# Waiting by tile instead of by pool, early query weights and expert sums in written order, in a two-layer gated cross-attention model

## The chip, the cores and the metric

The kernel runs on one core of a Trainium2 chip. The metric is the device time of one execution in microseconds, and a kernel's time is the median over several executions. Profiled times come from one recorded execution; positions such as "at 2477" are microseconds from the start of its span.

The engines are called by short names: PE is TensorE's matrix multiplication (PEld its weight load), DVE is VectorE, ACT is ScalarE, POOL is GpSimd, and SP is SyncE, whose queue only issues DMAs here. ACT and POOL issue DMAs too.

## What is computed

An input x of 1600 rows (16 sequences of 100) and 512 columns passes four gated stages, all in float32. The second operand is a context of 16 sequences of 722 rows and 384 columns:

```python
x = x + tanh(g_xattn[0]) * attention0(layernorm(x), ctx)   # 16 heads of 32
x = x + tanh(g_ffn[0])   * experts(layernorm(x))           # 8 experts, top 2
x = x + tanh(g_xattn[1]) * attention1(layernorm(x), ctx)   # 8 heads of 64
x = x + tanh(g_ffn[1])   * ffn(layernorm(x))
```

An attention projects x to queries and the context to keys and values, takes a softmax over the 722 context rows for each head, and projects the result back. The experts stage sends every row to its two best experts, each a silu-gated pair of 512x1024 matrices and one of 1024x512, and adds the two results by the weights of a softmax. The last stage normalizes its input again inside, keeps that input as its own residual, and runs a silu network of width 2048 whose weights are int32 numbers with a scale for each group of 128 rows:

```python
def ffn(x):
    h = layernorm(x) * gamma + beta
    w1 = (q1 - 128) * s1          # by groups of 128 rows
    y = silu(h @ w1 + b1)
    w2 = (q2 - 128) * s2
    return x + 0.5 * (y @ w2 + b2)
```

## The kernel before

**Tiles and stages.** The 1600 rows of x stay in SBUF as 13 tiles of up to 128 rows. The stages follow each other on the profile's axis: attention 0 (0 to 959), routing (959 to 1005), experts (1005 to 1633), attention 1 (1634 to 2460), the quantized network (2477 to 2848).

**Who sets the order.** Inside `tc.manual_schedule(engines={PE})` the order of PE's instructions is the order of the program. All other engines get theirs from a scheduler, which may move an instruction ahead of another where data allow. An instruction that `keep_in_program_order` marks stays in written order. So most of this kernel is a list of units written for PE, with the other engines' work placed around it. Buffers come from pools: a tile pool takes a stretch of SBUF or PSUM, and a pool that is opened where an earlier one stood has its first tiles wait for the earlier pool's users. A tag with `bufs=n` turns over n buffers.

**Attention.** `Attention.run` goes through 64 steps, one for each sequence b and each of four column blocks m. In a step PE makes the next step's scores (`ps_s`, L369), attends for the step before (`ps_r` L447 spreads the reciprocals of the softmax sums, `ps_pv` L460 multiplies by the values) and transposes this step's probabilities (`ps_t`, L428). DVE copies the negated scores with their minimum (`ns`, L379 in attention 1), ACT takes their exponential (`pr_a`, L411), and DVE and ACT share the copies of the transposed probabilities (`pT`, L435 and L437). DVE makes the reciprocals (`rinv`, L444) and the scaled result (`tT`, L467). Keys (`ps_k`, L207) and values (`ps_v`, L232) of later sequences fill PE between. `extra[step]` holds units for a given step: `query_input` normalizes a tile of x (`xn_a`, L306 on ACT or L116 on POOL) and transposes it (`ps_tr`, L131), `queries` multiplies by the query weights (`ps_q`, L329), and `project` makes the output (`ps_y`, L473) and adds it to x on DVE (L480). The list `more` gives attention 1 further units.

**Routing and experts.** `Experts` computes logits, the two best experts of every row and a sorted place for each, in a chain of small operations beside which PE makes values of attention 1. Then `slots` runs 29 slots of 128 sorted rows. A slot takes 21.6 us (628 us over 29), multiplies one tile through one expert (`hidden`, then `give`), and loads the weights for the slots ahead on SP's queue (L790 to L794): two of 1 MB for each half of the first pair, and 2 MB for the last matrix. ACT copies the result (`ot`) and writes it to `rows` in DRAM. A branch at L895 for further slots, and one at L1447 for a guarded attention, are not taken with this input.

**Entry to attention 1.** `load_query_weights` fetches Wq on SP (L273), `load_output_weights` fetches Wo on POOL (L282), `output_bias` scales the bias (L300). `combine` gathers a tile's two expert rows from DRAM by indirect DMAs on POOL (`r`, L914) and adds each to x on DVE (L920). `summed` adds that tile's mean and variance (L102, L103) and scales: a square root on ACT (L109), then a reciprocal and a shift on DVE. `sqrt` and `exp` need different tables on ACT, and a change of table shows as ACT_TABLE_LOAD. The first sum stands ahead of attention 1; `more` writes sums 1 to 3 at step 0, and sums 4 to 12 at steps 1 to 9.

**Quantized network.** `quantized_ffn` works on groups of 4, 3, 3 and 3 tiles. `weights` loads integers `q` (one buffer, L961 and L964) and scales into `ffn_w` (L962 and L965), and DVE makes the weights from them (L969). `normal` normalizes twice: POOL makes `xn_ffn` (L116), DVE adds it to x (L983) and takes its moments, POOL normalizes it again, in place. PE transposes it (`ps_hT`, L1004; sixteen transposes for a group of four tiles), DVE scales it (`hT`, L1009), and then PE alternates `ps_y` (L1026) and `ps_z` (L1044) to the end.

Of the kernel before, what the change touches and what calls it, by code (L numbers as in the profile page):

```python
# [8 lines left out]
F32 = mybir.dt.float32  # L9
I32 = mybir.dt.int32  # L10
AF = mybir.ActivationFunctionType
ALU = mybir.AluOpType
AX = mybir.AxisListType
PSUM = bass.MemoryType.PSUM
PE = mybir.EngineType.PE

P = 128
B, T, C = 16, 100, 512
# [30 lines left out]

def bcast(ap, *shape):  # L50
    return ap.to_broadcast(list(shape))


def rows_of(i):
# [80 lines left out]
class Attention:  # L135
# [16 lines left out]
    def open_first(self, ctx):  # L152

        tc, nc, name = self.net.tc, self.net.nc, self.name
        self.pa = ctx.enter_context(tc.tile_pool(name=f"{name}_a", bufs=1))
        self.pk = ctx.enter_context(tc.tile_pool(name=f"{name}_k", bufs=4))
        self.wk = self.pa.tile([P, KK, C], F32, name=f"wk_{name}")
        self.wv = self.pa.tile([P, KK, C], F32, name=f"wv_{name}")
        wk = self.w["Wk"].rearrange("(k p) m -> p k m", p=P)
        t = self.pa.tile([P, KK, S], F32, tag="ctx", bufs=2, name=f"ctx_{name}_0")  # L160
        cx = self.ctxT[0].rearrange("(k p) s -> p k s", p=P)
        for k in range(KK):
            nc.sync.dma_start(self.wk[:, k, :], wk[:, k, :])
            nc.sync.dma_start(t[:, k, :], cx[:, k, :])
        self.cxs[0] = t
        nc.sync.dma_start(self.wv, self.w["Wv"].rearrange("(k p) m -> p k m", p=P))
        if "bk_cols" in self.w:
            self.cols["bk"] = self.pa.tile([P, KC], F32, name=f"bkc_{name}")
            nc.gpsimd.dma_start(self.cols["bk"], self.w["bk_cols"])
# [77 lines left out]

    def open(self, ctx):
        tc, nc, name, w = self.net.tc, self.net.nc, self.name, self.w
        pool = lambda n, k, **kw: ctx.enter_context(  # L250
            tc.tile_pool(name=f"{name}_{n}", bufs=k, **kw)
        )
        self.pb, self.pw, self.p2 = pool("b", 1), pool("w", 1), pool("2", 2)
        self.p3, self.p4 = pool("3", 3), pool("4", 4)
        self.ps_s, self.ps_m = pool("s", 2, space=PSUM), pool("m", 4, space=PSUM)
        self.wq = self.pw.tile([P, KC, C], F32, name=f"wq_{name}")
        self.wo = self.pw.tile([P, KC, C], F32, name=f"wo_{name}")
        for n in ("bq", "bv"):
            if n + "_cols" in w:
                self.cols[n] = self.pw.tile([P, KC], F32, name=f"{n}c_{name}")  # L260
                nc.gpsimd.dma_start(self.cols[n], w[n + "_cols"])
        self.gbo = self.pw.tile([P, C], F32, name=f"gbo_{name}")

        self.tT = self.pw.tile([P, KC, N], F32, name=f"tT_{name}")
        self.probs = [
            self.pw.tile([T, NS * P], F32, name=f"pr{i}_{name}") for i in range(6 if self.G == 4 else 4)
        ]
        for t in self.probs:
            nc.gpsimd.memset(t[:, S:], 0.0)
        self.qT, self.nmax, self.sums, self.negated, self.pT = {}, {}, {}, {}, {}  # L270

    def load_query_weights(self):
        self.net.nc.sync.dma_start(self.wq, self.w["Wq"].rearrange("(k p) m -> p k m", p=P))  # L273

    def load_output_weights(self, queue, pin=False):

# [209 lines left out]
    def run(self, given, after_project=None, more=()):  # L486
# [9 lines left out]
        for g in range(1, B // GB):  # L496
            at = 4 * KC * (g - 1)
            for n, i in enumerate(range(last_tile(g - 1) + 1, last_tile(g) + 1)):
                extra[at + 2 + n].append((self.query_input, i))
            for m in range(KC):  # L500
                extra[at + 7 + 2 * m].append((self.queries, g, m))
        for b in range(B):
# [39 lines left out]
class Experts:  # L542
# [10 lines left out]
    def open(self, pc):  # L553
# [26 lines left out]
            )  # L580
            return t

        self.e_m8 = const_iota([P, NTT, E], [[0, NTT], [1, E]], -E, 0, "e_m8")
        self.j_rows = const_iota([P, E, CAP // P], [[0, E], [P, CAP // P]], 0, 0, "j_rows")
        self.count = const_iota([P, P], [[1, P]], 0, 0, "count")
        self.token = const_iota([P, 2, NTT], [[0, 2], [P, NTT]], 0, 1, "token")
        nc.gpsimd.memset(self.token[NL:, :, NTT - 1], 0.0)
# [41 lines left out]
    def top_two(self, i0, i1):  # L629

        nc, hot = self.net.nc, self.hot
        n, s = i1 - i0, slice(i0, i1)
        lg, at, first, e_m8 = self.lg[:, s], self.at[:, s], self.first[:, s], self.e_m8[:, s]
        for k in range(2):
            nc.vector.tensor_reduce(self.top[:, k, s], lg, AX.X, ALU.max)
            nc.vector.tensor_tensor(
                at, lg, bcast(self.top[:, k, s].unsqueeze(2), P, n, E), ALU.is_equal
            )
            nc.vector.tensor_tensor(at, at, e_m8, ALU.mult)
            nc.vector.tensor_reduce(first, at, AX.X, ALU.min)  # L640
            nc.vector.tensor_tensor(
                hot[:, k, s], e_m8, bcast(first.unsqueeze(2), P, n, E), ALU.is_equal
            )
            if k == 0:
                nc.vector.scalar_tensor_tensor(lg, hot[:, 0, s], -BIG, lg, ALU.mult, ALU.add)
        if i1 == NTT:

            nc.vector.memset(hot[NL:, :, NTT - 1, :], 0.0)
        nc.vector.tensor_tensor(self.sel[:, s], hot[:, 0, s], hot[:, 1, s], ALU.add)
        for i in range(i0, i1):  # L650
            nc.vector.tensor_tensor(
                self.before_tile[:, i + 1, :], self.before_tile[:, i, :], self.sel[:, i, :], ALU.add
            )
# [3 lines left out]
    def places(self, psum, pn):  # L657
# [11 lines left out]
        nc.vector.tensor_scalar(cnt, ps_n, float(CAP), None, ALU.min)  # L669
        more = pn.tile([P, E, CAP // P], F32, name="more")  # L670
        nc.vector.tensor_tensor(
            more, bcast(cnt.unsqueeze(2), P, E, CAP // P), self.j_rows, ALU.is_gt
        )
        ntile = pn.tile([P, E], F32, name="ntile")
        nc.vector.tensor_reduce(ntile, more, AX.X, ALU.add)
# [22 lines left out]
        for k in range(2):  # L698
# [8 lines left out]
        full = of_hot[:, :, :, 1:]  # L707
        nc.vector.tensor_tensor(
            full,
            bcast(rank.unsqueeze(3), P, 2, NTT, E - 1),  # L710
            bcast(self.j_rows[:, 0:1, 1:].unsqueeze(1), P, 2, NTT, E - 1),
            ALU.is_ge,
        )
        fulls = new("fulls")
# [55 lines left out]

    def open_weights(self, ctx, n):

        self.pw[n] = ctx.enter_context(self.net.tc.tile_pool(name=f"moe_w{n}", bufs=1))

    def load(self, j, part, again=False):

# [18 lines left out]

    def open_slots(self, ctx):
        tc = self.net.tc
        pool = lambda n, k, **kw: ctx.enter_context(tc.tile_pool(name=f"moe_{n}", bufs=k, **kw))
        self.p2 = pool("2", 2)
        self.ps_h, self.ps_t = pool("h", 4, space=PSUM), pool("t", 2, space=PSUM)  # L800
        self.ps_o = pool("o", 2, space=PSUM)

    def open_rows(self, ctx):
        self.px = ctx.enter_context(self.net.tc.tile_pool(name="moe_x", bufs=2))

    def gather(self, j, again=False):
        if not again:
# [19 lines left out]
    def hidden(self, j, part):  # L827
# [5 lines left out]
        for n in range(2):  # L833
# [8 lines left out]
                        stop=(k == KC - 1),  # L842
                    )
            phs.append(ph)
        s = self.p2.tile([P, n4, P], F32, tag="silu", name="silu")
        nc.scalar.activation(s, phs[0], AF.Silu)
        m = self.p2.tile([P, n4, P], F32, tag=f"midT{part}", name=f"midT{part}_{j}")
        nc.vector.tensor_tensor(m, s, phs[1], ALU.mult)  # L848
        self.midT[j, part] = m

    def give(self, j):
# [4 lines left out]
        for f in range(KF):  # L856
# [4 lines left out]
                start=(f == 0),  # L861
                stop=(f == KF - 1),
            )
        ot = self.p2.tile([P, C], F32, tag="ot", name=f"ot_{j}")
        nc.scalar.copy(ot, po)
        nc.scalar.dma_start(self.rows[j * P : (j + 1) * P, :], ot)

# [42 lines left out]
    def combine(self, pg, i):  # L910
        net, nc, n = self.net, self.net.nc, rows_of(i)
        for k in range(2):
# [4 lines left out]
                in_=self.rows[:, :],  # L917
                in_offset=bass.IndirectOffsetOnAxis(ap=self.slot_i[:n, k, i : i + 1], axis=0),
            )
            nc.vector.scalar_tensor_tensor(  # L920
                net.x[:n, i, :],
                r[:n, :],
                self.probs[:n, k, i : i + 1],
# [2 lines left out]
                ALU.add,  # L926
            )


def quantized_ffn(net, p, gate, out):  # L930

    nc, tc, x = net.nc, net.tc, net.x
    out = out.rearrange("b t c -> (b t) c")
    with ExitStack() as ctx:
        pool = lambda n, k, **kw: ctx.enter_context(tc.tile_pool(name=f"ffn_{n}", bufs=k, **kw))

        ps, pq, p1, px, ph, p2 = (
            pool("s", 1), pool("q", 1), pool("1", 1), pool("x", 4), pool("h", 2), pool("2", 2),
        )
        ps_t, ps_y, ps_z = (pool(n, k, space=PSUM) for n, k in (("t", 2), ("y", 2), ("z", 4)))  # L940
        small = {}
# [381 lines left out]
def tile_flamingo(ctx: ExitStack, tc: tile.TileContext, a: dict, out: bass.AP):  # L1323
# [21 lines left out]
    with ExitStack() as cm:  # L1345
# [58 lines left out]
        with ExitStack() as c1:  # L1404
# [3 lines left out]
            with ExitStack() as cw:  # L1408
                moe.open_weights(cw, 0)
                moe.open_rows(cw)  # L1410
                with ExitStack() as cr:
                    ps = cr.enter_context(tc.tile_pool(name="route_p", bufs=6, space=PSUM))
                    p2 = cr.enter_context(tc.tile_pool(name="route_2", bufs=2))
                    pn = cr.enter_context(tc.tile_pool(name="route_n", bufs=1))
                    a1.ps_m = ps
                    units = a1.keys_and_values(0)

# [29 lines left out]
                with tc.If(nc.values_load(flag[0:1, 0:1], min_val=0, max_val=1) > 0):  # L1447
                    guarded_attention(net, a["x"], a["ctxT"], w0, tgx[:, 0:1], heads, o_s, x_s)
                    with ExitStack() as cg:
# [17 lines left out]
                            moe.gather(j, again=True)  # L1467
                        moe.weigh()
                        moe.turn_rows(0, ps, again=True)
                with ExitStack() as cs:  # L1470
                    moe.open_weights(cs, 1)
                    moe.open_slots(cs)
                    moe.slots({3: [(a1.load_ctx, 2, True)]})

            a1.open(c1)
            a1.load_query_weights()
            pg = c1.enter_context(tc.tile_pool(name="moe_g", bufs=4))

            def summed(i):
                moe.combine(pg, i)  # L1480
                net.moments(i)
                net.norm_scales(i, i + 1)

            more = []
            for i in range(1, 4):
                more += [(0, summed, i), (1, a1.query_input, i, True), (3, a1.add_bias, i)]
            more += [(3, a1.add_bias, 0)]
            more += [(2, a1.queries, 0, m, T, GT) for m in range(KC)]
            more += [(i - 3, summed, i) for i in range(4, NTT)]
            with tc.manual_schedule(engines={PE}):  # L1490
                summed(0)
                a1.load_output_weights(nc.gpsimd, True)
                a1.output_bias()
                units = a1.keys_and_values(1)[:NS]
                for f, *u in units[:3]:
                    f(*u)
# [65 lines left out]
```

## Time and profile before

| | |
|---|---|
| median of 3 runs | 2849.27 us (2849.23 to 2851.45) |
| profiled execution | 2849.85 us |
| its span | 2848.1 us, mean granted TensorE clock 0.991 |
| PE busy | 2795.5 us, 98% |
| DVE busy | 867.5 us, 30% |
| ACT busy | 864.8 us, 30% |
| POOL busy | 170.6 us, 6% |

"Busy" is the time in which an engine executes instructions; issuing a DMA doesn't count. The profile has several views. The groups list instructions of one line with their count and mean time. The waits list for each engine what ended its idle time, as "instruction <- what it waited for: us in total, times, longest". The chain of waits goes back from the last instruction to what released it. The timeline lists instructions by start time, with start, duration, engine, line, operation, output and inputs, and in square brackets the engine's idle time before and who ended it; a trailing x4 means four of them merged in one row, so that a row's duration is that of all. Table rows of stretches of time give the granted clock, where 1.00 is full speed.

### The profile page before, as it was taken

What the parts mean: (1) busy time and instruction counts of PE and PEld (TensorE: products, weight loads), DVE (VectorE), ACT (ScalarE), POOL (GpSimd) and SP (SyncE); (2) the same over time, 40 slices, a digit from 0 to 9 for tenths busy, and PEclk for the clock granted to TensorE, in tenths of its full rate; (3) what the DMA queues carried; (4) which work ended last, traced back from release to release, by engine and by line L of the source; (5) the groups of instructions that cost most, each with busy time, mean ns of one, the idle gap of its engine ahead of it and who ended that gap; (6) DMA issues with size and microseconds to landing.
All of it is one profiled execution on the core that took longest, in us unless ns stands there. A gap on an engine that the chain in (4) does not pass through costs nothing. (4 is left out here: it accounts for less than half of the span.)

```text
span 2848.1 us, 42495 instructions
## 1 busy us (share of the span) xinstructions
PE 2795.5 (98%) x18000; PEld 1739.8 (61%) x18000; DVE 867.5 (30%) x2569; ACT 864.8 (30%) x1724; POOL 170.6 (6%) x187
## 2 busy tenths in 40 slices
PE   9999999999999999999999979999999999799999
PEld 4555555555556588888788745555555555444554
DVE  4444444444445500000000072233232322521100
ACT  2544454454455310000000033233333333211110
POOL 2000000000000000000000050000000000301000
PEclk9999999999999999999999989999999999899999
DMA  4000000001000489899889441000000000420000
GB/s 160 17 17 17 33 24 24 17 28 33 17 28 1 151 333 330 316 320 320 315 312 320 149 129 32 16 16 32 16 16 32 17 32 1 140 96 15 11 12 9
DMA packets 129880, 278.10 MB, mean 98 GB/s; under 512 B 5824, under 2 KB 5840, under 8 KB 129168
## 3 DMA queue, kind: packets, MB, share of 16 engines
q1 hardware_dynamic: 117888, 246.80, 24.9%
q0 software_dynamic: 5088, 16.28, 1.7%
q10 hardware_dynamic: 6704, 12.19, 1.1%
q8 instruction: 145, 2.38, 0.3%
q14 instruction: 55, 0.45, 0.0%
HBM read 260.31 MB, written 14.94 MB: 97 GB/s over the span
## 5 line engine op out<-in xcount | busy, mean ns | idle before, releaser
L232 PE MATMUL ps_v<-wv_a,ctx_a 128*128 128x512 f32 (+1 forms) x1152 | 524.8, 600 | 2.5 <-ACTq L895 1.6
L207 PE MATMUL ps_k<-ctx_a,wk_a 128*128 128x361 f32 x1488 | 488.6, 473 | 0.0
L837 PE MATMUL ps_h<-xT,w 128*128 128x128 f32 x3712 | 421.1, 276 | 3.7 <-DVEq L1447 3.7
L837 PEld LDWEIGHTS ps_h<-xT,w 128*128 128x128 f32 x3712 | 418.6, 193 | 4.4 <-issue 4.4
L207 PEld LDWEIGHTS ps_k<-ctx_a,wk_a 128*128 128x128 f32 x1488 | 271.9, 190 | 150.4 <-issue 13.5
L232 PEld LDWEIGHTS ps_v<-wv_a,ctx_a 128*128 128x128 f32 (+1 forms) x1152 | 204.7, 185 | 236.9 <-issue 227.2
L392 DVE TENSOR_SCALAR_CACHE_REDUCE ns<-ps_s 100x361 f32<-100x361 f32 x512 | 246.8, 529 | 208.3 <-PE ps_s L369 185.8
L428 PEld LDWEIGHTS ps_t<-ident,pr_a 100*128 100x128 f32 x2304 | 214.0, 141 | 80.5 <-issue 41.6
L411 ACT ACTIVATE pr_a<-ns,extremes 100x722 f32<-100x722 f32 x256 | 227.1, 889 | 71.7 <-DVE extremes L402 71.7
L428 PE MATMUL ps_t<-ident,pr_a 100*128 100x100 f32 x2304 | 237.3, 252 | 1.5 <-DVE rb L455 1.1
L437 DVE COPY pT<-ps_t 128x400 f32<-128x400 f32 x288 | 163.5, 571 | 241.2 <-PE ps_t L428 235.4
L369 PE MATMUL ps_s<-kT_a,qT_a 32*100 32x361 f32 (+1 forms) x1536 | 212.3, 500 | 7.4 <-DVE ns L379 4.8
L239 ACT COPY v_a<-ps_v 128x512 f32<-128x512 f32 x192 | 111.5, 581 | 346.5 <-PE ps_v L232 346.1
L857 PE MATMUL ps_o<-w,midT 128*128 128x512 f32 x464 | 203.9, 592 | 0.0
L379 DVE TENSOR_SCALAR_CACHE_REDUCE ns<-ps_s 100x722 f32<-100x722 f32 x128 | 111.3, 907 | 281.1 <-PE ps_s L369 281.1
L1044 PE MATMUL ps_z<-ffn_w,y_ffn 128*128 128x512 f32 (+1 forms) x416 | 190.8, 594 | 0.0
L435 ACT COPY pT<-ps_t 128x400 f32<-128x400 f32 x288 | 141.3, 492 | 158.7 <-PE ps_t L428 149.2
L1026 PE MATMUL ps_y<-hT,ffn_w 128*128 128x384 f32 (+2 forms) x512 | 184.1, 504 | 0.0
L848 DVE TENSOR_TENSOR midT<-silu,ps_h 128x512 f32<-128x512 f32 x58 | 39.9, 688 | 388.7 <-PE ps_h L837 376.6
L369 PEld LDWEIGHTS ps_s<-kT_a,qT_a 32*100 32x100 f32 (+1 forms) x1536 | 73.7, 161 | 137.9 <-issue 91.4
L460 PE MATMUL ps_pv<-pT,v_a 128*32 128x100 f32 (+3 forms) x4608 | 156.2, 249 | 0.4 <-DVE pT L437 0.3
L1026 PEld LDWEIGHTS ps_y<-hT,ffn_w 128*128 128x128 f32 x512 | 95.4, 190 | 84.9 <-issue 49.9
(161 smaller groups left out, 1849.5 us busy)
## 6 DMA issues: line engine op xcount, KB each, us to landing
w<-in_L_ffn_w SPq DMA_DIRECT2D x116, 1024.0 KB, 6.7
w<-in_L_ffn_wo SPq DMA_DIRECT2D x29, 2048.0 KB, 11.1
ctx_a<-in_ctxT SPq DMA_DIRECT2D x30, 1083.0 KB, 5.3
q<-in_L_ffn_fc_q SPq DMA_DIRECT2D x8, 1024.0 KB, 5.4
ffn_w<-in_L_ffn_fc_scales SPq DMA_DIRECT2D x8, 1024.0 KB, 11.5
rows<-ot ACTq DMA_DIRECT2D x29, 256.0 KB, 8.8
xn_d<-xn_moe ACTq DMA_DIRECT2D x12, 256.0 KB, 2.0
ctx_a<-in_ctxT SPq DMA_DIRECT2D x6, 361.0 KB, 5.8
```

The lines of the kernel that those rows point to most:

```text
L207: nc.tensor.matmul(ps, self.wk[:, k, m * P : (m + 1) * P], self.cxs[b][:, k, c * SH : (c + 1) * SH], start=(k == 0), stop=(k == KK - 1),)
L232: nc.tensor.matmul(ps[:n], self.cxs[b][:, k, c * P : c * P + n], self.wv[:, k, :], start=(k == 0), stop=(k == KK - 1),)
L369: nc.tensor.matmul(pss[n // 2][:, n % 2, :SH], self.qT[g][j * D : (j + 1) * D, m, q], self.kT[b, m][j * D : (j + 1) * D, c * SH : (c + 1) ...
L392: nc.vector.tensor_scalar(self.negated[b, m][j][:, part * SH : (part + 1) * SH], pss[j // 2][:, j % 2, :SH], -1.0, BIG, ALU.mult, ALU.min, ...
L411: nc.scalar.activation(self.prob(b, h)[:, :S], ns, AF.Exp, bias=self.nmax[b][:, h : h + 1], scale=-1.0, accum_out=self.sums[b][:, h : h + 1],)
L428: nc.tensor.transpose(ps[:, i, :], self.prob(b, m * G + 2 * pair + j)[:, c * P : (c + 1) * P], self.net.ident[:T, :T],)
L437: nc.vector.tensor_copy(to, ps)
L460: nc.tensor.matmul(ps[j * D : (j + 1) * D, :], self.v[b][:n, c, m * P + j * D : m * P + (j + 1) * D], self.pT[b, m, j // 2][:n, j % 2 * NS ...
L837: nc.tensor.matmul(ph[:, f, :], w[:, n, k, f * P : (f + 1) * P], self.xT[j][:, k, :], start=(k == 0), stop=(k == KC - 1),)
L857: nc.tensor.matmul(po, self.midT[j, f // 4][:, f % 4, :], w[:, f, :], start=(f == 0), stop=(f == KF - 1),)
L1026: nc.tensor.matmul(ps[:, :nt], w1[f // nf][:, k, f % nf * P : (f % nf + 1) * P], hT[g][:, k, :nt], start=(k == 0), stop=(k == KC - 1),)
L1044: nc.tensor.matmul(z[j][:n], y[:, j * P : j * P + n], w2[f // nf][:, f % nf, :], start=(f == 0), stop=(f == NF - 1),)
```

## The change

The change has these parts.

- Nearly every pool is opened by a new helper, `open_pool`, with `reuse_waits="tile"`: a new tile waits for the users of those old tiles whose memory it takes, and no longer for the whole old pool. The order of pools in the quantized network is changed as well.
- The query weights of attention 1 get a pool of their own on the right side of SBUF, opened ahead of the slots. They are fetched on SP's queue in expert slot 3, behind a load of context, and held in written order there.
- In `slots`, `silu` and `ot` get one buffer instead of two, and so does `midT` of part 1. Two constants of the routing are held once and broadcast where they were held repeated.
- `query_input` for later groups is written one step later, in both attentions.
- The DVE sums of `combine` are held in written order. Sum 1 is written at step 0, sums 2 and 3 at step 1, and sums 4 to 12 at steps 2 to 10. The loads of Wo and of the output bias, and the scaling of that bias, move from ahead of attention 1 to step 1. `query_input` of tiles 2 and 3 moves to step 2.

```diff
+def open_pool(ctx, tc, name, bufs=1, **kw):
+
+    return ctx.enter_context(tc.tile_pool(name=name, bufs=bufs, reuse_waits="tile", **kw))
...
-        self.pa = ctx.enter_context(tc.tile_pool(name=f"{name}_a", bufs=1))
-        self.pk = ctx.enter_context(tc.tile_pool(name=f"{name}_k", bufs=4))
+        self.pa = open_pool(ctx, tc, f"{name}_a")
+        self.pk = open_pool(ctx, tc, f"{name}_k", 4)
...
-        self.wq = self.pw.tile([P, KC, C], F32, name=f"wq_{name}")
+        if not hasattr(self, "wq"):
+            self.wq = self.pw.tile([P, KC, C], F32, name=f"wq_{name}")
...
-    def load_query_weights(self):
-        self.net.nc.sync.dma_start(self.wq, self.w["Wq"].rearrange("(k p) m -> p k m", p=P))
+    def load_query_weights(self, pin=False):
+
+        net = self.net
+        ins = net.nc.sync.dma_start(self.wq, self.w["Wq"].rearrange("(k p) m -> p k m", p=P))
+        if pin:
+            net.tc.keep_in_program_order(ins)
...
-                extra[at + 2 + n].append((self.query_input, i))
+                extra[at + 3 + n].append((self.query_input, i))
...
-        self.e_m8 = const_iota([P, NTT, E], [[0, NTT], [1, E]], -E, 0, "e_m8")
-        self.j_rows = const_iota([P, E, CAP // P], [[0, E], [P, CAP // P]], 0, 0, "j_rows")
+        self.e_m8 = const_iota([P, E], [[1, E]], -E, 0, "e_m8")
+        self.j_rows = const_iota([P, CAP // P], [[P, CAP // P]], 0, 0, "j_rows")
...
-        s = self.p2.tile([P, n4, P], F32, tag="silu", name="silu")
+        s = self.p2.tile([P, n4, P], F32, tag="silu", name="silu", bufs=1)
...
-        m = self.p2.tile([P, n4, P], F32, tag=f"midT{part}", name=f"midT{part}_{j}")
+        m = self.p2.tile([P, n4, P], F32, tag=f"midT{part}", name=f"midT{part}_{j}", bufs=2 - part)
...
-        ot = self.p2.tile([P, C], F32, tag="ot", name=f"ot_{j}")
+        ot = self.p2.tile([P, C], F32, tag="ot", name=f"ot_{j}", bufs=1)
...
-            nc.vector.scalar_tensor_tensor(
+            ins = nc.vector.scalar_tensor_tensor(
                 net.x[:n, i, :],
                 r[:n, :],
...
+            net.tc.keep_in_program_order(ins)
...
-        ps, pq, p1, px, ph, p2 = (
-            pool("s", 1), pool("q", 1), pool("1", 1), pool("x", 4), pool("h", 2), pool("2", 2),
+        ps, pq, px, ph, p1, p2 = (
+            pool("s", 1), pool("q", 1), pool("x", 4), pool("h", 2), pool("1", 1), pool("2", 2),
         )
...
+                pr = open_pool(c1, tc, "a1_q", side="right")
+                a1.wq = pr.tile([P, KC, C], F32, name="wq_a1")
                 with ExitStack() as cs:
                     moe.open_weights(cs, 1)
                     moe.open_slots(cs)
-                    moe.slots({3: [(a1.load_ctx, 2, True)]})
+                    moe.slots({3: [(a1.load_ctx, 2, True), (a1.load_query_weights, True)]})

             a1.open(c1)
-            a1.load_query_weights()
-            pg = c1.enter_context(tc.tile_pool(name="moe_g", bufs=4))
+            pg = open_pool(c1, tc, "moe_g", 4)
...
-            more = []
-            for i in range(1, 4):
-                more += [(0, summed, i), (1, a1.query_input, i, True), (3, a1.add_bias, i)]
-            more += [(3, a1.add_bias, 0)]
+            more = [(0, summed, 1), (1, a1.query_input, 1, True), (1, summed, 2), (1, summed, 3)]
+            more += [(2, a1.query_input, i, True) for i in (2, 3)]
             more += [(2, a1.queries, 0, m, T, GT) for m in range(KC)]
-            more += [(i - 3, summed, i) for i in range(4, NTT)]
+            more += [(1, a1.load_output_weights, nc.gpsimd, True), (1, a1.output_bias)]
+            more += [(3, a1.add_bias, i) for i in range(4)]
+            more += [(i - 2, summed, i) for i in range(4, NTT)]
             with tc.manual_schedule(engines={PE}):
                 summed(0)
-                a1.load_output_weights(nc.gpsimd, True)
-                a1.output_bias()
```

The remaining lines of the diff open other pools by the same helper and put the broadcasts of `e_m8` and `j_rows` where these are used.

More of the change, by code (lines that the diff above doesn't have):

```diff
@@ L249, in open @@
         tc, nc, name, w = self.net.tc, self.net.nc, self.name, self.w
-        pool = lambda n, k, **kw: ctx.enter_context(
-            tc.tile_pool(name=f"{name}_{n}", bufs=k, **kw)
-        )
+        pool = lambda n, k, **kw: open_pool(ctx, tc, f"{name}_{n}", k, **kw)
         self.pb, self.pw, self.p2 = pool("b", 1), pool("w", 1), pool("2", 2)
@@ L632, in top_two @@
         n, s = i1 - i0, slice(i0, i1)
-        lg, at, first, e_m8 = self.lg[:, s], self.at[:, s], self.first[:, s], self.e_m8[:, s]
+        lg, at, first = self.lg[:, s], self.at[:, s], self.first[:, s]
+        e_m8 = bcast(self.e_m8.unsqueeze(1), P, n, E)
         for k in range(2):
@@ L671, in places @@
         nc.vector.tensor_tensor(
-            more, bcast(cnt.unsqueeze(2), P, E, CAP // P), self.j_rows, ALU.is_gt
+            more,
+            bcast(cnt.unsqueeze(2), P, E, CAP // P),
+            bcast(self.j_rows.unsqueeze(1), P, E, CAP // P),
+            ALU.is_gt,
         )
@@ L709, in places @@
             full,
-            bcast(rank.unsqueeze(3), P, 2, NTT, E - 1),
-            bcast(self.j_rows[:, 0:1, 1:].unsqueeze(1), P, 2, NTT, E - 1),
+            bcast(rank.unsqueeze(3), P, 2, NTT, CAP // P - 1),
+            bcast(self.j_rows[:, 1:].unsqueeze(1).unsqueeze(1), P, 2, NTT, CAP // P - 1),
             ALU.is_ge,
@@ L771, in open_weights @@
     def open_weights(self, ctx, n):
-        self.pw[n] = ctx.enter_context(self.net.tc.tile_pool(name=f"moe_w{n}", bufs=1))
+        self.pw[n] = open_pool(ctx, self.net.tc, f"moe_w{n}")
     def load(self, j, part, again=False):
@@ L797, in open_slots @@
         tc = self.net.tc
-        pool = lambda n, k, **kw: ctx.enter_context(tc.tile_pool(name=f"moe_{n}", bufs=k, **kw))
+        pool = lambda n, k, **kw: open_pool(ctx, tc, f"moe_{n}", k, **kw)
         self.p2 = pool("2", 2)
@@ L803, in open_rows @@
     def open_rows(self, ctx):
-        self.px = ctx.enter_context(self.net.tc.tile_pool(name="moe_x", bufs=2))
+        self.px = open_pool(ctx, self.net.tc, "moe_x", 2)
     def gather(self, j, again=False):
@@ L934, in quantized_ffn @@
     with ExitStack() as ctx:
-        pool = lambda n, k, **kw: ctx.enter_context(tc.tile_pool(name=f"ffn_{n}", bufs=k, **kw))
-        ps, pq, p1, px, ph, p2 = (
-            pool("s", 1), pool("q", 1), pool("1", 1), pool("x", 4), pool("h", 2), pool("2", 2),
+        pool = lambda n, k, **kw: open_pool(ctx, tc, f"ffn_{n}", k, **kw)
+        ps, pq, px, ph, p1, p2 = (
+            pool("s", 1), pool("q", 1), pool("x", 4), pool("h", 2), pool("1", 1), pool("2", 2),
         )
@@ L1411, in tile_flamingo @@
                 with ExitStack() as cr:
-                    ps = cr.enter_context(tc.tile_pool(name="route_p", bufs=6, space=PSUM))
-                    p2 = cr.enter_context(tc.tile_pool(name="route_2", bufs=2))
-                    pn = cr.enter_context(tc.tile_pool(name="route_n", bufs=1))
+                    ps = open_pool(cr, tc, "route_p", 6, space=PSUM)
+                    p2 = open_pool(cr, tc, "route_2", 2)
+                    pn = open_pool(cr, tc, "route_n")
                     a1.ps_m = ps
```

## The prediction

> **What bounds the kernel now.** The page's first table says who is busy:
>
> ```profile
> PE 2795.5 (98%) x18000; PEld 1739.8 (61%) x18000; DVE 867.5 (30%) x2569; ACT 864.8 (30%) x1724; POOL 170.6 (6%) x187
> ```
>
> TensorE works 98% of the span, everything else a third or less, and the change takes no matmul away. What can be won is the 52.6 us in which PE stands (2848.1 - 2795.5)[...]. Next, PE's waits:
>
> ```profile
> PE ps_hT L1004 <- POOL xn_ffn L116: 17.7, 4, 16.8
> PE ps_tr L131 <- ACT xn_a L306: 6.0, 1, 6.0
> PE ps_s L369 <- DVE ns L379: 4.8, 1, 4.8
> ...
> PE ps_tr L131 <- DVE qT_a L342: 3.4, 1, 3.4
> ...
> PE ps_v L232 <- DVE x L480: 0.8, 1, 0.8
> ```
>
> Five waits, 33 us, all at stage boundaries: the FFN's entry (16.8), the second attention's entry (6.0, 4.8, 3.4) and routing's (0.8). No wait names an expert weight. The timeline at the FFN's entry:
>
> ```profile
> 2436.93 0.37 SPq L961 DMA_DIRECT2D q<-in_L_ffn_fc_q  x1
> ...
> 2452.93 7.28 PE L473 MATMUL ps_y<-wo_a,tT_a 128*128 128x512 f32 x16
> ...
> 2460.36 0.37 SPq L962 DMA_DIRECT2D ffn_w<-in_L_ffn_fc_scales  x1
> ...
> 2460.46 4.57 POOL L116 TENSOR_SCALAR xn_ffn<-x,rstd,shift 128x512 f32<-128x512 f32 x4 [348.88 <-PE ps_y L473]
> ...
> 2470.25 2.29 DVE L969 SCALAR_TENSOR_TENSOR ffn_w<-q,ffn_w 128x2048 f32<-128x2048 int32 x1 [1.59 <-issue]
> ...
> 2477.03 0.47 PE L1004 MATMUL ps_hT<-ident,xn_ffn 128*128 128x128 f32 x1 [16.82 <-POOL xn_ffn L116]
> ```
>
> POOL's normalization and the scales' DMA both start just after attention's last projection ends (2460.21), though the rows were final long before: both wait for a pool, not for data. The second attention's entry:
>
> ```profile
> 1642.79 1.58 DVE L920 SCALAR_TENSOR_TENSOR x<-r,probs,x 128x512 f32<-128x512 f32 x2 [16.21 <-DMA r<-rows,slot_i]
> 1645.39 1.28 ACT L109 ACT_TABLE_LOAD   x1 [7.59 <-DVE mean L103]
> 1648.27 1.11 PE L131 MATMUL ps_tr<-ident,xn_a 128*128 128x128 f32 x4 [5.99 <-ACT xn_a L306]
> ...
> 1668.25 0.90 DVE L379 TENSOR_SCALAR_CACHE_REDUCE ns<-ps_s 100x722 f32<-100x722 f32 x1
> ...
> 1669.21 3.56 PE L369 MATMUL ps_s<-kT_a,qT_a 64*100 64x361 f32 x8 [4.85 <-DVE ns L379]
> ```
>
> The first sum waits for its gathers; then PE waits for a softmax step (ns) that stands on DVE behind sums of later tiles.
>
> [...] granted clock 0.50 in 1650-1652, 1670-1676 and 2465-2482. [...] The load is 1.28 here, [...] the one at 1682.02 starts 0.01 after ACT's copies end, so I count 1.28. [...] a sum takes 0.73 alone, 2.28 at 1658.25 beside POOL's add.
>
> **The change part by part.**
>
> *Tile waits, routing.* The first ps_v waits for its own tile only: +0.83 (gains are positive).
>
> *Tile waits, FFN entry.* POOL's first xn pass then waits for the last ps_k of attention (2436.85) and can run at once; the scales are issued behind the first q, about 2437.3. But the changed program's order puts this work into the last two attention steps: three x<-xn_ffn (0.75 each) stand on DVE ahead of step 62's ns, four bn_stats (0.66) ahead of step 63's copies, and three of the sixteen ps_hT transposes on PE behind the last-but-one step's ps_pv. Stepping the queues by hand, attention's tail stalls 1.4 at ps_r and 1.8 at ps_t (their rinv and rb are late on DVE), and 2.1 at ps_hT (POOL's second pass comes at 2453.1 to 2454.7); with 3 x 0.27 for the transposes it ends at 2466.3, not 2460.2 (+6.1). The other thirteen take 3.6, to 2469.9. Dequantization of w1_0 stands on DVE behind the last hT (0.83) and two x<-xn of the next tiles (0.75 each): 2472.2 to 2474.5. ps_y starts then, after a gap of 4.6. w2_0's q still waits for that dequantization (one buffer): 2474.5 + 5.3 to land (page's 5.4) = 2479.8, dequantized (2.28) by 2483.1. First ps_z at 2483.1 against 2489.9 in the chain of waits: +6.8. Bounds +4 (half clock after the gap[...]) to +13 (no tail stall: 6.8 + 6.1).
>
> *wq early.* Its 1 MB rides on SP in expert slot 3 behind a context load. A slot is 21.6 us (628 us by 29); expert weights there are issued about 36 us ahead and land in 6.7 to 11.1, so 3 us more is covered; if that cover were gone, 3 us. POOL's gathers lose wq's traffic: the first gathers took up to 7.2 us to land beside wq and wo, the median is 3.8. I take the first sum's second half 2.1 sooner: ps_tr at 1646.15 instead of 1648.27.
>
> *Sums one a step, in order.* With most sums gone from DVE's queue, ps_s(0) runs at 1660.2 and its ns at 1661.4 instead of 1668.3: the 4.85 wait goes, and scores, ps_t and the next scores end at 1667.0, where they ended at 1677.6. Now what is late next. ps_r needs a reciprocal that stands on DVE behind sum 1 (held to written order, so it waits for its gathers) and the next step's two ns (0.90 each): until 1671.3, a gap of 4.3. ps_tr of tile 1 needs xn_1, which stands on ACT behind exp, load, sqrt, load, exp (1.09 + 1.28 + 0.30 + 1.28 + 1.09, then 0.81 for itself): until 1676.0, a gap of 3.1 after ps_r and ps_pv. Attending and scoring go on to 1680.9. xn_2 and xn_3 stand behind the next such pair of loads: until 1687.1 (6.1) and 1689.9 (2.2). The remaining queries start at 1691.3 instead of 1684.6, but tile and scores that followed before come ahead of them now, and their own qT wait (3.42) is gone: the ps_s after them starts at 1706.2 against 1703.7, and one ps_tr (0.63) is still owed: -3.1, wq's 2.1 included. Bounds +1.5 (ACT takes xn first) to -6 (half clock through 1671-1680). Output weights and gbo move behind six more gathers on POOL (about 0.97 each to issue), to about 1669; the first projection, five steps in, needs them: covered. gbo's scaling waits on DVE for that DMA until about 1675; behind it stand copies of pT and, on POOL, add_bias: inside the gaps counted.
>
> *Steady steps.* Nine sums (4 to 12, steps 2 to 10) now each put a sqrt between exps: 9 x 2 x 1.28 = 23 us more on ACT, in steps of 12.9 us (826 by 64) where ACT is busy 3 tenths. Behind the loads stand exp and pT copies, and PE's ps_t and ps_pv for them. Every chain I stepped closes in under 12.7; I take -0.5, bounds 0 and -23.
>
> *The rest at nothing.* bufs=1 for silu, ot, midT1: reused 21 us later, read within 8.8. query_input one step later: same transposes, tiles wanted 4 steps on. Smaller constants: the routing chain hides behind filled-in ps_v (bounds ±0.5).
>
> Sum: 0.8 + 6.8 - 3.1 - 0.5 = **4.0 us**. The profiled execution took 2849.85 (span 2848.1 and 1.75 around it), giving 2845.85. The median is 0.58 below that execution: 2849.27 - 4.0 = 2845.3.
>
> **The rivals.** Measurement tells about 0.2%, 5.7 us, from no change.
>
> *A, the FFN entry pays in full:* DVE has the room and the tail doesn't stall (its 30% busy speaks for it; the order with x<-xn ahead of ns against): 12.9 + 0.8, attention's entry even: 2835.6. Chance 0.2.
>
> *B, table loads in the steady steps:* ns waits for a sum, sum for its gather, exp for two loads, and PE for exp. It decides from 1.1 us a step: nine steps x 1.1 = 10 us turn 2845.3 into 2855. With 1.5 us of the 2.56 exposed (13.5, less the 0.5 counted) it is 2858; with all, 2868. For it: ps_t already waited behind a load at 1668-1672. Against: scores run one step ahead, ACT is 70% idle. Chance 0.2.
>
> *C, the tile waits do not free the FFN:* the new tiles lie on memory released last, so only entry costs remain: 0.8 - 3.1 - 0.5, 2852. Against: the order on POOL shows the wait on ps_k. Chance 0.1.
>
> *Forecast:* 0.5, own range 2841 to 2850.
>
> **How the numbers follow.** Under 2843.6 lies A, and 0.15 of the forecast's 0.5: faster 0.35. Above 2855: most of B, little of C: slower 0.2. Between: 0.45. The range leaves out a part of A below and the worse part of B above: 2835 to 2857.
>
> **What would show it.** Right: no 16.8 wait at ps_hT, first ps_z some 7 us nearer to the last attention matmul of before; ps_r and ps_tr waiting on DVE and ACT in 1667-1690, sqrt loads once a step. Wrong: waits spread over steps 2 to 10 (B), ps_hT still waiting over 10 us (C), or attention's tail undisturbed (A).

## The result, and the profile after

The changed kernel is slower, by 0.2%: its median is 2856.01 us (2848.37 to 2859.15, 12 runs) against 2849.25 us before (2847.35 to 2851.45, 12 runs), a ratio of 1.0020 with a 95% interval of 1.0012 to 1.0028. The forecast was 4.0 us faster. The time also spreads more than before, and the spread goes with the granted TensorE clock: the fastest run has a mean clock of 0.992, the slowest 0.987. The profiled execution is that slowest one, 2859.15 us with a span of 2857.4, so it shows some 3 us more loss than the median.

The waits of PE, in the changed kernel's profile (line numbers are 5 to 14 higher than before):

```profile
PE ps_tr L136 <- ACT xn_a L314: 15.4, 4, 6.0
PE ps_y L1040 <- DVE ffn_w L983: 5.2, 1, 5.2
...
PE ps_r L455 <- DVE rinv L452: 3.2, 1, 3.2
...
PE ps_s L377 <- DVE ns L387: 1.0, 1, 1.0
...
PE ps_hT L1018 <- POOL xn_ffn L121: 0.6, 2, 0.3
```

The 16.8 us at ps_hT are gone, so are 3.8 of the 4.8 at ps_s. In their place stand waits at ps_tr, ps_r and ps_y. PE stands still for 49.0 us in all (2857.4 minus the busy time below), 3.6 less than before. Yet its busy time rose by 12.9 us for the same 18000 matmuls. This is the first table of the page:

```profile
PE 2808.4 (98%) x18000; PEld 1748.7 (61%) x18000; DVE 865.9 (30%) x2569; ACT 887.1 (31%) x1742; POOL 169.4 (6%) x187
```

With less standing and a longer busy time for the same matmuls goes a lower mean granted clock, 0.987 against 0.991 before: PE worked more of its time at half clock (a granted clock of 0.50). To see where, I took the start of the same matmuls in both traces, after minus before, and how this difference grows over each stretch:

| stretch | growth, us |
|---|---|
| start, to 100 | +1.6 |
| end of attention 0 (the wait for x at L480) | -0.9 |
| routing, up to the first expert | +3.5 |
| experts | 0.0 |
| first value matmul of attention 1 | -1.2 |
| entry of attention 1, from there to 1720 | +7.7 |
| steps of attention 1 after 1720 | +1.0 |
| FFN's entry | -2.4 |
| FFN | 0.0 |
| sum | +9.3, the difference of the spans |

The first and third rows are stages in which the two kernels give PE the same matmuls; there the stretches at a granted clock of 0.50 are longer after the change (3.4 us lost instead of 1.7 at the start, 6.8 instead of 3.4 in routing; a stretch's loss is its length times 1 minus its clock). At the start the loss is anything from 0 to 3.4 us over the twelve versions that were profiled. In routing it goes with the version: between 940 and 1020, 5.1 or 6.8 us are lost in all nine that have the tile waits and the smaller constants there, and 3.4 in all three that don't. No run changes that stage alone. Entry and FFN are the change's own.

At the entry, in the timeline of the changed kernel:

```profile
1675.79 0.60 PE L455 MATMUL ps_r<-ident,rinv 100*64 100x100 f32 x4 [3.23 <-DVE rinv L452]
1675.81 1.28 ACT L114 ACT_TABLE_LOAD   x1
...
1677.10 0.29 ACT L114 ACTIVATE rstd<-mean,eps 128x1 f32<-128x1 f32 x1
1677.41 1.28 ACT L419 ACT_TABLE_LOAD   x1
...
1679.60 0.80 ACT L314 ACTIVATE xn_a<-x,shift,rstd 128x512 f32<-128x512 f32 x1
1680.45 1.12 PE L136 MATMUL ps_tr<-ident,xn_a 128*128 128x128 f32 x4 [2.06 <-ACT xn_a L314]
...
1692.92 1.11 PE L136 MATMUL ps_tr<-ident,xn_a 128*128 128x128 f32 x4 [5.35 <-ACT xn_a L314]
```

ACT goes from exponential to square root and back, with 1.28 us of table loading each way, before it reaches the xn_a that PE waits for. The granted clock around there is the last number but two of these rows, PE's busy time the first after the length. First the kernel before:

```profile
1665.00:1680.00 15.00, 10.79 (x65) 6.89 (x66) 11.90 (x29) 7.15 (x14) 5.39 (x6) 0.66 0.36 103
1680.00:1695.00 15.00, 14.23 (x98) 10.39 (x95) 14.01 (x40) 9.47 (x18) 12.55 (x11) 1.00 0.29 80
1695.00:1710.00 15.00, 12.13 (x74) 7.92 (x75) 10.03 (x26) 5.20 (x11) 3.59 (x4) 0.89 0.12 28
```

Then the changed kernel, which reaches the entry 3.0 us later:

```profile
1665.00:1680.00 15.00, 9.17 (x66) 5.78 (x65) 9.25 (x25) 9.27 (x17) 3.29 (x4) 0.86 0.38 123
1680.00:1695.00 15.00, 8.23 (x56) 5.75 (x56) 10.64 (x24) 8.51 (x13) 8.69 (x7) 0.61 0.21 58
1695.00:1710.00 15.00, 13.17 (x49) 9.65 (x50) 3.30 (x8) 1.30 (x2) 1.32 (x2) 0.73 0.04 14
```

And at the FFN's entry, in the timeline:

```profile
2448.63 4.56 POOL L121 TENSOR_SCALAR xn_ffn<-x,rstd,shift 128x512 f32<-128x512 f32 x4 [315.79 <-PE ps_k L212]
...
2462.83 0.56 PE L436 MATMUL ps_t<-ident,pr_a 100*128 100x100 f32 x4 [1.14 <-DVE rb L463]
...
2468.31 2.26 PE L436 MATMUL ps_t<-ident,pr_a 100*128 100x100 f32 x12
...
2486.47 2.69 DVE L983 SCALAR_TENSOR_TENSOR ffn_w<-q,ffn_w 128x2048 f32<-128x2048 int32 x1
...
2489.21 10.00 PE L1040 MATMUL ps_y<-hT,ffn_w 128*128 128x512 f32 x16 [5.24 <-DVE ffn_w L983]
```

POOL starts right behind the last key matmul, as forecast. But a group of twelve ps_t takes 2.26 us, at a granted clock of 0.50 (2466 to 2474). It takes 1.25 us at a clock of 1.00 (2450 to 2454) in the same place of a version below that keeps the old order of the sums:

```profile
2451.79 1.25 PE L436 MATMUL ps_t<-ident,pr_a 100*128 100x100 f32 x12
```

So the end of attention's tail runs at half clock here.

### The profile page after: what moved, and what is told of

Read it like the earlier page. It is cut to its first block, busy times and chain, and to the rows that moved or that the text cites. A ratio compares the mean times of both kernels' runs of the same rounds, so it can differ in the third digit from the quotient of the medians.

```text
span 2857.4 us, 42455 instructions
## 1 busy us (share of the span) xinstructions
PE 2808.4 (98%) x18000; PEld 1748.7 (61%) x18000; DVE 865.9 (30%) x2569; ACT 887.1 (31%) x1742; POOL 169.4 (6%) x187
```

## The experiments

Each version was timed beside the kernel before, and each ratio is to that session's before, whose median lay between 2849.25 and 2851.19 us. A difference between versions of different sessions can therefore be off by some 2 us.

**The new order of the sums alone.** The kernel before with the new list and the held sums; the rest is as before.

```diff
-                more += [(0, summed, i), (1, a1.query_input, i, True), (3, a1.add_bias, i)]
-            more += [(i - 3, summed, i) for i in range(4, NTT)]
+            more = [(0, summed, 1), (1, a1.query_input, 1, True), (1, summed, 2), (1, summed, 3)]
+            more += [(i - 2, summed, i) for i in range(4, NTT)]
...
+            net.tc.keep_in_program_order(ins)
```

> The kernel before with only the new order of the expert sums (held in written order, one tile a step, output weights loaded at step 1). Theory 1, the new order at attention 1's entry is the loss: the waits at ps_r and ps_tr and the half-clock stretches behind them come without tile waits, and it is 5 to 8 us slower than before, 2854 to 2857. Theory 2, the loss lies in what the tile waits place in attention's last two steps and in half-clock stretches elsewhere: within 1 us of before, 2848 to 2850.

Measured: 2882.98 us, ratio 1.0115 (1.0100 to 1.0131). Slower, as theory 1 says, but by 33 us, four times its figure. PE's waits in its profile tell why:

```profile
PE ps_tr L131 <- ACT xn_a L306: 16.1, 4, 6.0
PE ps_tr L131 <- POOL xn_a L116: 15.2, 3, 5.8
```

The first row is the changed kernel's own wait. The second is new: three waits of 4.9, 4.4 and 5.8 us at 1713 to 1747, where POOL normalizes tiles 4 to 6 for the next group of queries. Their sums have only just been made, and POOL issues the next gathers first. The changed kernel doesn't have them, and one of its edits must hide them.

**Everything but the new order of the sums.** The changed kernel with the old list, nothing held.

> The changed kernel with the old order of the expert sums (not held, three tiles at step 0, output weights ahead of attention); tile waits, early query weights and the FFN's pools stay. Theory 1: without the new order the gain of the FFN's entry (2.4 us in the changed kernel's profile) and of routing (0.9) stands alone, 2844 to 2847. Theory 2: it keeps the loss, 2854 to 2857.

Measured: 2844.65 us, ratio 0.9981 (0.9973 to 0.9988), 5.6 us under before. Theory 1 holds. In its profile, the fastest of its 16 runs, the entry of attention 1 gains 3.6 us, where it loses 6.5 in the changed kernel (both with the first value matmul). The new order costs 11.4 us in all (2856.01 to 2844.65).

**Tile waits alone.** Before, with `open_pool` and the FFN's order of pools. The smaller constants of routing are in it too, which the expectation doesn't name.

> The kernel before with tile waits and the FFN's order of pools only: sums, query weights, query_input and the experts' buffers as before. Theory 1: 2845 to 2848, and up to 2 us over the version with early query weights, if these make the first gathers faster. Theory 2: slower than before, 2853 or more.

Measured: 2844.02 us, ratio 0.9976 (0.9969 to 0.9983). Early query weights, single buffers and the later query_input thus bring nothing that can be told under the old order of the sums: the version with them is 0.6 us slower. The smaller constants were not measured by themselves.

**No table loads at the sums.** In the changed kernel, which then leaves out the square root:

```diff
-        nc.scalar.activation(r, m[:, :, 1], AF.Sqrt, bias=self.eps)
+        nc.scalar.activation(r, m[:, :, 1], AF.Identity, bias=self.eps)
```

> The changed kernel with ACT's identity in place of the square root in the scales of the expert sums: the square root is left out, every instruction keeps its place, and ACT has no table to load between exponentials. Theory 1a, the waits at ps_tr in attention 1's entry stand on the table loads: the two waits for xn_1 and xn_2 shrink by 2 to 3 us each, less half-clock follows, 2849 to 2852. Theory 1b, they stand on the order of DVE (sums and statistics before what PE waits for): within 1.5 us of the changed kernel's 2856.

Measured: 2848.32 us, ratio to before 0.9999 (0.9990 to 1.0007), 7.7 us under the changed kernel. From 1660 to 1850 its trace shows no table load, the changed kernel's 23 of 1.28 us each. Theory 1a holds, though 0.7 us outside its range: table loads are the larger part, 7.7 of the 11.4 us, of what the new order costs. But the waits shrink by less than it says:

```profile
PE ps_tr L146 <- ACT xn_a L324: 11.2, 3, 4.7
...
PE ps_r L465 <- DVE rinv L462: 3.2, 1, 3.2
```

The two longest, 6.0 and 5.35 us, become 4.7 and 3.9; that for xn_1 goes, that for xn_3 grows from 2.0 to 2.6; ps_r still waits 3.2 us for rinv. So DVE's order (1b) keeps its share. The waits at ps_tr lose 4.2 us together; over 1660 to 1780 the half clock takes 6.8 us instead of 11.9 (sum of 1 minus the clock over stretches of 2 us, PE's idle time included). These profiles are the fastest of 13 runs here and the slowest of 12 there, so these differences are larger than those between typical runs.

A version that keeps the root, made on DVE, was meant for the same question and has no time; whether the loads can be avoided at this gain stays open.

**query_input at its old place.** In the changed kernel:

```diff
-                extra[at + 3 + n].append((self.query_input, i))
+                extra[at + 2 + n].append((self.query_input, i))
```

> The changed kernel with query_input at its old place, one step earlier. Theory 1: the later sums leave a tile's normalization only that one step, so the three waits of 4.4 to 5.8 us at ps_tr for POOL's xn_a in steps 2 to 4, and the half-clock behind them, come back: 20 to 25 us slower than the changed kernel, 2876 to 2881. Theory 3, those waits come from the pools: no change, 2855 to 2858.

Measured: 2877.45 us, ratio to before 1.0094 (1.0079 to 1.0110), 21.4 over the changed kernel. The three waits are back, as in the first experiment:

```profile
PE ps_tr L136 <- POOL xn_a L121: 15.2, 3, 5.8
```

Theory 1 holds. The one line that seemed to cost and bring nothing is what makes the new order bearable.

**The first four sums as before, the rest held.** In the changed kernel:

```diff
+            more = []
+            for i in range(1, 4):
+                more += [(0, summed, i), (1, a1.query_input, i, True), (3, a1.add_bias, i)]
+            more += [(3, a1.add_bias, 0)]
...
+            if i > 3:
+                net.tc.keep_in_program_order(ins)
```

Wo and the bias are loaded ahead of attention again, and sums 4 to 12 stay at steps 2 to 10.

> The changed kernel with the sums of tiles 0 to 3, Wo and the bias in their old order and not held; only the sums of tiles 4 to 12 are held, one a step from step 2. Theory 1: what costs is holding and delaying the first four; what the held order wins, a DVE free for the first softmax (the wait of 4.9 us at ps_s), comes from the later nine. No wait over 3 us at ps_r, ps_tr or ps_s after the first tile's, and 4 to 7 us under the version with all sums in old order: 2838 to 2841. Theory 4, holding the later sums costs by itself (table loads in each step): 2850 or more.

Measured: 2834.24 us, ratio 0.9953 (0.9939 to 0.9966), almost 4 us under the expected range. At the entry one wait over 1.0 us is left, the first tile's:

```profile
PE ps_tr L136 <- ACT xn_a L314: 6.0, 1, 6.0
```

This splits the new order's 11.4 us: what it does with the first four sums and the loads of Wo and the bias costs 21.8 (2856.01 to 2834.24), and what it does with the later nine wins 10.4 (2844.65 to 2834.24). Whether these nine win by being held or by coming a step later was not separated. From 1700 to 1850 ACT still loads a table 15 times (17 times in the changed kernel, once before), 1.28 us each time, so theory 4 falls: the loads in the steps are covered.

**The first weights ahead of hT.** The version before this, and:

```diff
+            with tc.issue_after(made[0].ins):
+                for k in range(KC):
+                    turn(0, FG[0], k)
```

Here `made[0]` is the first dequantization; the next group's `normal` is wrapped in the same way.

> The one before with the FFN's first dequantization put ahead of hT and of the next group's x<-xn on DVE. The weights landed long before. Theory: the wait of 5.2 us of PE at ps_y for ffn_w shrinks to 2 to 3, w2_0's integers are issued as much sooner, and it is 2 to 5 us under the one before, 2834 to 2838. Rival: hT is late instead, by the same 2.3 us, and the time is the same within 1 us.

Measured: 2829.66 us, ratio 0.9926 (0.9913 to 0.9940), 4.6 us less, as much as the theory says. PE's 5.2 us at ps_y are gone, 3.0 at ps_hT have come:

```profile
PE ps_tr L136 <- ACT xn_a L314: 6.0, 1, 6.0
...
PE ps_hT L1020 <- DVE hT L1025: 3.0, 1, 3.0
```

The rival was half right: hT is late now, its wait grown from 0.9 us to 3.0, but by less than the weights were.

**Tile waits in the FFN alone.** The kernel before with `reuse_waits="tile"` and the new order of pools in `quantized_ffn`.

> The kernel before with tile waits and the new order of pools in the quantized FFN alone. It measures the disputed term of the prediction by itself: a gain of 6.8 us at the FFN's entry was forecast, and the changed kernel's profile showed 2.4. Theory 1, the waits are as forecast and the clock of attention's tail decides: between 2.4 and 6.8 on average over the runs, 2843 to 2848, with first ps_z earlier than in the kernel before. Rival: the tail's new stalls eat the gain, 2849 to 2851.

Measured: 2846.90 us, ratio 0.9985 (0.9978 to 0.9992): 4.3 us faster, by the interval 2.3 to 6.3. Theory 1 holds. In its profile the first ps_z comes 50.8 us after the last ps_k (52.9 before), and the same twelve ps_t of the tail take 2.26 us: the clock falls to 0.50 in the tail here too (2454 to 2462), without the new order of the sums.

**The first tile behind more values.** On top of the weights-first version:

```diff
-                for f, *u in units[:3]:
+                for f, *u in units[:5]:
                     f(*u)
                 a1.query_input(0, True)
```

> The version with the first four sums free and the weights first, with query_input of tile 0 behind five of the six units of values (ps_v) instead of behind three. PE's wait of 6.0 us for the first tile's xn_a was in all runs so far. Theory: two more units (about 5.3 us at full clock) cover it, the half-clock after it goes too, and it is 6 to 9 us under that version, 2821 to 2824. Rival: the first tile's copy and queries then come later and their own waits take its place, within 2 us of 2829.7.

Measured: 2829.74 us, ratio 0.9924 (0.9911 to 0.9938), nothing gained. The rival was right, and the waits show the place:

```profile
PE ps_q L337 <- DVE mean L108: 6.1, 1, 6.1
...
PE ps_tr L136 <- ACT xn_a L314: 1.0, 1, 1.0
```

PE no longer waits for the tile, but 6.1 us for its copy. The row names `mean`, but what ps_q reads is the copy, which ends 0.15 us before ps_q starts; it stands on DVE behind the next sums and statistics.

**The copy first.** There, `issue_after` puts sums 1 to 3 and the bias behind the first tile's copy on DVE.

> The version with query_input of tile 0 behind five units, with the first tile's copy put ahead of the bias and of sums 1 to 3 on DVE. In the version before this the wait of 6 us moved from ps_tr to ps_q, whose tile's copy stood on DVE behind sums that waited for their gathers. Theory: with the copy first, both waits go, 5 to 8 us under 2829.7, 2822 to 2825. Rival: the sums delayed by it make qT or ns late, and the time stays within 2 us of 2829.7.

Measured: 2824.99 us, ratio 0.9911 (0.9895 to 0.9928). Both waits are gone (ps_tr keeps 0.9 us); of 6 us, 4.7 come out. Part of the rest is what the rival feared: the wait for ns at ps_s grows from 1.0 us to 2.3. It is the best version of the study, 25.7 us under the kernel before.

## Why the prediction was wrong

The step that failed is the clock. The prediction stepped FFN's entry and the sums' order at full clock and left the half clock to its bounds. The runs show half clock where it had none, and both terms came out lower, as did a third, the early wq, for another reason. Term by term, in the changed kernel's profile:

**Routing, +0.8.** The wait of 0.83 us for x is gone, as forecast. But routing takes 3.5 us more there, with 6.8 us lost to half clock (0.50 from 990 to 1000), and no version with the tile waits of this stage lost less than 5.1 us to it (3.4 before). The prediction put routing's clock at nothing. Whether the tile waits cause the loss is not shown.

**FFN's entry, +6.8.** The path is right, the size only at full clock. From the end of the last ps_k to the first ps_z the prediction has 46.2 us (2483.1 minus 2436.85), before has 52.9. One profile, with the old sums, shows 46.5. There attention's tail ends 5.3 us later than before (forecast 6.1), by stalls of 0.9 at ps_t, 0.7 at ps_r and 1.1 at ps_t and three early ps_hT, and PE waits 5.2 (forecast 4.6) at ps_y. That the end agrees so well is partly luck. The forecast's last wait, for w2_0, doesn't show: ps_y starts behind the gap at a granted clock of 0.50 (2470 to 2474), takes 9.79 us (7.29 before), and ends after w2_0 is ready. The forecast's own steps (2479.8 and 2.28) end at 2482.1, too, not 2483.1.

In the changed kernel's profile the stretch is 50.5 us with the same waits and the same instructions; what differs is that its tail ran at 0.50 from 2466 to 2474. This is not the new sums' doing. Of the seven profiles with these pools and the weights in this place, five have such a tail and 50.3 to 50.8 us, tile waits alone and FFN alone among them; the other two have 46.5 and 47.5. The mis-sized term is "half clock after the gap" as a bound only: in these five profiles the clock falls before the gap, in the tail itself (to 0.50, in 2450 to 2458 with tile waits alone), and the gain is 2.1 to 2.6 us. Alone, this part gives 4.3 us in the median.

**wq early, 2.1 of the entry.** Wrong. The gathers did land in 2.9 to 3.9 us instead of up to 7.2. But the step before them was not looked at: POOL clears four pr_a tiles first, and in the changed kernel's trace a value matmul of the entry (PE ps_v) is what ends their wait, at 1640.21. The first gather was issued 4.4 us after the first value matmul (1641.67 minus 1637.29), not 2.1 (1636.35 minus 1634.29). With tile waits alone and Wq late, the first gather waits for a ps_v as well (2.87 us), so this comes with the tile waits. The wait for the first tile stayed at 5.99 us.

**The sums' order, -3.1 with wq.** Every wait that the prediction named is there: ps_r 3.2 us (forecast 4.3), then xn_1 2.1 (3.1), xn_2 5.4 (6.1), xn_3 2.0 (2.2); and the wait for ns shrank to 1.0, that for qT went. The waits were sized 3 us too long, and still the loss was too small: the entry lost 6.5 us, all its parts together. The step that failed is the choice of full clock behind them, with the half clock "through 1671-1680" left to the bound. In the trace the clock is 0.61 in 1680-1695 and 0.73 in 1695-1710, and the 32 ps_q of the remaining queries run there. Four waits, none over 5.4 us, stand between 1672.6 and 1696.1, and the clock is 0.50 from 1676 to 1686 and from 1690 to 1702: the half clock takes 15.4 us from the entry, 10.3 before. Taking the table loads away gave back 7.7 us, giving the first four sums, Wo and the bias their old place 21.8.

**query_input one step later, nothing.** The time of this edit is not zero: without it the changed kernel loses 21.4 us more. The prediction costed it against the old sums, where the tile was ready long before. Beside the new list, sum 4 is made at step 2, and step 2 is also where it would be used.

**Steady steps, -0.5.** Near: 1.0 us of loss. Rival B, the table loads in the steady steps, falls: fifteen such loads stand in the 2834.24 us version. Rival A's size was not seen; the FFN entry with the clock full in its tail gained 6.4 us, half of A's 12.9. Rival C falls too: ps_hT waits 0.6 us for POOL.

The prediction's "five waits" pass over two of 4.7 us (ps_k for the first context) and 3.7 (ps_h at the first expert). The change leaves both as they are, at 4.5 and 3.9.

So in this profile routing's 0.9 and FFN's 2.4 us are gained and 6.5 and 1.0 lost, 4.2 in all; the other 5.1 of its 9.3 are the longer half-clock stretches of the start and of routing. A forecast of 4.0 us less became a median of 6.8 more.

## What to carry to other kernels

Where PE is the bound, cost a cluster of short waits by the granted clock around it, not by the waits alone: with the four waits behind the first tile's (12.6 us) the entry lost 15.4 us to half clock, without them 3.4. And when a producer moves later, list every consumer that was written for its old time. Delaying and holding work paid where slack is large (sums 4 to 12) and was dear where PE is waiting already (sums 0 to 3). A wait taken away can go one instruction further, as from ps_tr to ps_q and from ps_y to ps_hT here, so look at the queue's order at both places at once.

## What the runs showed of the hardware

In two places the clock fell without any long wait. These rows are of the kernel before, in routing, while 52 narrow matmuls (ps_map, 128x32) run back to back for 5.89 us from 985.78:

```profile
988.00:990.00 2.00, 2.00 (x20) 2.00 (x19) 0.00 (x0) 0.00 (x0) 0.00 (x0) 1.00 1.05 408
990.00:992.00 2.00, 2.00 (x16) 1.78 (x16) 0.19 (x1) 0.00 (x0) 0.00 (x0) 0.93 1.05 403
992.00:994.00 2.00, 2.00 (x5) 1.16 (x4) 0.00 (x0) 0.00 (x0) 1.51 (x2) 0.50 1.02 388
```

PE is busy for all of each row, and the clock is 0.50 at the end. It falls here in all eleven profiles that were read in rows of 2 us: 1.00 in 984 to 986, 0.50 in a row between 988 and 994. Attention's tail in the changed kernel shows the like: PE is busy 57% to 85% of each 2 us from 2454 to 2466 with no wait over 1.2 us, and the clock is 0.58 in 2464 to 2466 and 0.50 from there to 2474. In the same tail it stayed at 1.00 in one profile with the old sums (2446 to 2468) and fell to 0.50 in two others with them (tile waits alone, 2450 to 2458; FFN alone, 2454 to 2462).

The time lost at half clock (summed as above) is near a multiple of 1.7 us in each stage summed, in these eleven profiles, and none of these 44 sums is more than 0.1 us away: none, 1.7 or 3.4 at the start, 3.4, 5.1 or 6.8 in routing, and at the entry 10.3 (before), 15.4 (changed) and 3.4 (first four free). What sets this step, and why the clock falls while PE is busy, in one profile and not in the next, was not tried.
